# Three fixed tiles, used in turn, for the sums and tangents of an additive attention layer

## The chip, the cores and the metric

The kernel runs on one core of a Trainium2 chip. The core has five engines that run their own instruction streams[...]: TensorE (PE, with its weight loads as PEld), VectorE (DVE), ScalarE (ACT), GpSimd (POOL) and SyncE (SP, which here issues the DMAs). The metric is the device time of one execution in microseconds, the median of several runs.

## The reference

A four-layer network over `x` of shape (4, 56, 56, 128): neighbourhood attention, a selective-scan block, then layer 2 and layer 3, each an attention and a mixture of experts over the 3136 tokens of an image. The change lies in the attention of layer 2, which is additive: a score is a weighted sum of 16 tangents, not a dot product.

```python
def _L2_attn_ref(x, W1, b1, w2, b2):              # x: normalized tokens (4, 3136, 128)
    f = einsum('bih,ha->bia', x, W1[:h])          # queries, a = 16
    g = einsum('bjh,ha->bja', x, W1[h:])          # keys
    t = tanh(f[:, :, None, :] + g[:, None, :, :] + b1)
    scores = einsum('bija,a->bij', t, w2[:, 0]) + b2[0]
    e = exp(scores) * tril(ones, -1)              # key j strictly before query i
    w = e / (sum(e, axis=-1, keepdims=True) + 1e-10)
    return einsum('bij,bjh->bih', w, x)           # then t = t + this
```

So every pair of a query and an earlier key of the same image needs 16 sums, 16 tangents and a weighted sum of them.

## The kernel before, in words

All in float32. The four images stay in SBUF (`X0` to `X3`, 28 tiles of 112 tokens each). Layer 2's attention (`layer2_attention`, L1139) works on one image after the other, and in an image on four chunks of 7 query tiles (784 queries). For a chunk, all keys up to its own last tile are gone through, one key tile `J` of 112 keys at a time, and each key tile in two halves. A half of a key tile is a *piece*; there are 560.

A piece holds 56 keys as 7 groups of 8 keys. In SBUF the 128 partitions of the tile `th` are 8 keys times 16 values of `a`, and its 7 x 784 elements per partition are 7 *slots* (one per group of keys) of 784 queries. A piece goes through four steps:

- `adds` (L1290), DVE: 7 instructions, one per slot, each writes slot `s` as the queries `fT` plus one column of keys `g` (L1297). On pieces whose keys lie among the chunk's own queries (the diagonal) only the columns `lo:hi` of each slot that come after the keys are made, so the instructions become narrower from 784 to 56 columns.
- `tangents` (L1302), ACT: one instruction takes the tangent of all 7 slots in place (L1306).
- `scores` (L1308), PE: for each slot and each half of 392 queries one matmul with the small matrix `place` sums over `a` with the weights `w2` and adds the rows of these keys to the PSUM tile `s` (L1320). The order is: slots 0 to 3 on the first 392 queries, slots 0 to 3 on the second, slots 4 to 6 on the first, slots 4 to 6 on the second. Where only the second half of the queries is left, it is slots 0 to 3, then 4 to 6.
- once both halves of a key tile are there: `weights` (L1329), ACT, takes the exponential (L1334, on the diagonal L1337), on the diagonal POOL multiplies by the mask `later` (L1341), and `weighted` (L1343), PE, adds the keys' tokens to the output `o` (L1350).

The order is written out by hand: the pools are under a manual schedule for PE, ACT, DVE and POOL, so each engine runs in the order of the program, and only SP's order is the scheduler's. For piece `i` the loop (L1435) issues: `tangents(i)`; perhaps one or two steps of background work (`deal`: normalizing and projecting the next chunk, the previous image's experts); `add_ahead(i + 2)`, which is `adds` of the piece two ahead; before the first half of a key tile `gather`, which is `weighted` of the key tile two before; `scores(i)`; after the second half `weights` of the key tile before. So DVE works two pieces ahead of ACT, and PE follows ACT in the same piece.

The tile `th` is made anew for each piece from the pool `sm` with three buffers (L1294). A new tile takes the buffer of the tile three pieces before. It may be written when the earlier tile has had its last access, whichever slot that was: the first of the seven adds of piece `i` waits for the last of the fourteen matmuls of piece `i - 3`. Before the seventh add the program then has no other wait on PE.

Where the tiles lie also matters in two places. The pools of layer 2 are opened in the order `l2_w`, `l2_big`, `l2_sm` (L1146 to L1153) and take the room that layer 1 gave back; layer 3's pools (L1798 on) take the room of layer 2 in the same order, beginning with the router's and the experts' weights `rw`, `ew`, `ew_last`, `rw_last` and the matrix `back` (L1800 to L1820). A tile of a later layer waits until the tiles that lay in its place have had their last access. By the addresses in the program of before, `ew` lies over `wf`, `wg` and the first of `l2_big`'s tiles, `xa` and `xT`; the three buffers of `th` lie behind all of `l2_big`, after `fT`.

Of the kernel before, what the change touches and what calls it, by code (L numbers as in the profile page):

```python
# [20 lines left out]
P = 128  # L21
TP = 2 * HW
# [35 lines left out]
NG = TP // JG  # L58
QW = 32

WT = 7
# [77 lines left out]
class Hybrid:  # L139
# [999 lines left out]
    def layer2_attention(self):  # L1139
# [5 lines left out]
        with ExitStack() as ctx:  # L1145
# [6 lines left out]
            big = ctx.enter_context(tc.tile_pool(name="l2_big", bufs=1, reuse_waits="tile"))  # L1152
            sm = ctx.enter_context(tc.tile_pool(name="l2_sm", bufs=2, reuse_waits="tile"))  # L1153
# [9 lines left out]
            self.psum2 = m, hold  # L1163
            pools = self.f2_wide, self.f2_sm, lambda: self.psum2[0](), lambda: self.psum2[1]()
            root = lambda var: self.rstd(sm, var, [TP, NT], 1e-5, "ln", bufs=1)
            im, fT, po, ps, th, es = {}, {}, {}, {}, {}, {}
            g, xk = {}, {}
            bind = lambda f, *args: lambda: f(*args)
# [10 lines left out]
            def span(j, J, half=0):  # L1179

                t, n = chunks[order[j][1]]
                return max(J - t, 0) * TP + (half * TP // 2 if J >= t else 0), n * TP
# [100 lines left out]
            def rounds(half):  # L1283

                return [
                    [(blk, 2 * half + q) for blk in range(3)] + ([(3, half)] if q == 0 else [])
                    for q in range(2)
                ]

            def adds(i):  # L1290
                j, J, half = pieces[i]
                lo, hi = span(j, J, half)
                b = order[j][0]
                th[i] = self.t(sm, [P, NG // 2, WT * TP], "th", bufs=3)  # L1294
                for s, (blk, q) in enumerate(sum(rounds(half), [])):
                    at = NG * (J % WT) + NG // 2 * half + 2 * blk + (q % 2 if blk < 3 else 0)
                    nc.vector.tensor_scalar(  # L1297
                        th[i][:, s, lo:hi], fT[j][:, lo:hi], g[b, J // WT][:, at : at + 1],
                        None, op0=ALU.add,
                    )  # L1300
# [90 lines left out]
            def add_ahead(i):  # L1391
                if i < len(pieces):
                    j = pieces[i][0]
                    if i == first[j] and j:
                        while now or later_on:
                            assert not state.held
                            run((now or later_on).pop(0))
                    adds(i)
# [808 lines left out]
```

## Time and profile before

| what | value |
|---|---|
| time, median of 3 runs | 7028.35 us (7022.07 to 7032.54) |
| the profiled execution's own time | 7027.59 us |
| its span, first to last instruction | 7025.8 us |
| DVE, ACT, PE busy over the span | 5763.3, 4832.9, 6054.1 us |
| layer 2's pieces, first add to last score | 3002.8 to 5601 us of the span |
| tangents, L1306 | 560, 2184.2 us; a full one 4785 ns |
| sums, L1297 | 3920, 1868.9 us; a full one 623 ns, of which the next covers the end |
| scores' matmuls, L1320 | 14112 rows, 1391.6 us |

Every matmul of float32 shows as two rows, so a full piece of 14 matmuls has 28. In the timeline view rows of one kind that follow each other without a gap are merged: "x28" on DVE is 28 instructions in one unbroken row. In the brackets stands how long the engine was idle before the row and what ended that. The view of waits gives, for an engine and a line, what it waited for: us in total, times, the longest. An engine's idle time costs nothing unless the engine that sets the pace waits in its turn.

### The profile page before, as it was taken

How to read it: one execution, taken by the hardware profiler on the slowest of the kernel's cores; microseconds unless marked ns; L12 is line 12 of the kernel's file. 1: busy time of each engine (PE TensorE's matmuls, PEld its weight loads, DVE VectorE, ACT ScalarE, POOL GpSimd, SP SyncE). 2: the span in 40 equal slices, each digit the busy share in tenths (PEclk: the TensorE clock that was granted, in tenths of full speed). 3: DMA queues.
4: the chain of work that ended last, by engine and by line, in shares of the span. 5: the costliest groups of instructions: out<-in, count | busy, mean ns of one | idle time of the engine just before them, and what ended most of it. 6: DMA issues, size and time to landing. Idle time of an engine off the chain costs nothing.

```text
span 7025.8 us, 101491 instructions
## 1 busy us (share of the span) xinstructions
PE 6054.1 (86%) x37386; PEld 2622.7 (37%) x37386; DVE 5763.3 (82%) x10108; ACT 4832.9 (69%) x4828; POOL 2849.9 (41%) x1921
## 2 busy tenths in 40 slices
PE   8889999999999999877777777777788799999998
PEld 7633333333233233232233323332333355555554
DVE  6879999999999999977878888888887753566665
ACT  5567667776766777589989998999899833322231
POOL 2369989998999999811010001000101100000000
PEclk9989989999999899889999999999899999999999
DMA  3057767777776777600000000000003304243433
GB/s 53 5 139 187 187 165 186 184 178 175 188 185 171 176 189 187 153 8 3 1 6 3 8 2 6 4 6 3 6 20 116 89 18 149 72 109 92 118 85 94
DMA packets 363447, 654.19 MB, mean 93 GB/s; under 512 B 95413, under 2 KB 211909, under 8 KB 362438
## 3 DMA queue, kind: packets, MB, share of 16 engines
q1 hardware_dynamic: 362949, 647.71, 36.9%
q8 instruction: 295, 4.83, 0.3%
q14 instruction: 203, 1.66, 0.1%
HBM read 536.78 MB, written 104.37 MB: 91 GB/s over the span
## 4 chain that ended last, share of the span: by engine, by line
PE 23%; ACT 12%; DVE 11%; issue 8%; POOL 1%; SPq 0%; DMA 0%; DVEq 0%; ACTq 0%; POOLq 0%
ACT th L1306 10%; PE o L1944 6%; DVE th L1297 6%; PE q L1932 5%; PE s L1320 5%; DVE X L2144 2%; PE pe L2139 2%; ACT e L1334 1%; POOL e L1341 1%; PE o L1350 1%; PE m L1478 1%; PE m L1253 1%; DVE wide L1964 1%; DVE X L1486 0%; PE m L1761 0%
## 5 line engine op out<-in xcount | busy, mean ns | idle before, releaser
L1306 ACT ACTIVATE th<-th 128x5488 f32<-128x5488 f32 (+13 forms) x560 | 2184.2, 3943 | 175.4 <-DVE th L1297 151.4
L1297 DVE TENSOR_SCALAR th<-fT,g 128x784 f32<-128x784 f32 (+13 forms) x3920 | 1868.9, 549 | 307.2 <-PE s L1320 286.5
L1320 PE MATMUL s<-th,place 128*32 128x392 f32 (+5 forms) x14112 | 1391.6, 488 | 442.2 <-ACT th L1306 439.5
L860 DVE TENSOR_TENSOR_SCAN hs<-E,u 128x896 f32<-128x896 f32 x728 | 1449.7, 2007 | 3.6 <-ACT E L844 3.6
L844 ACT ACTIVATE E<-E,rate 128x448 f32<-128x448 f32 x1456 | 886.0, 661 | 121.9 <-DMA E<-delta_dram 118.4
L865 POOL TENSOR_TENSOR hs<-hs,room 128x896 f32<-128x896 f32 x448 | 924.8, 2083 | 82.9 <-DVE hs L860 82.5
L865 POOL TENSOR_TENSOR hs<-hs,bc 128x896 f32<-128x896 f32 x448 | 926.5, 2087 | 47.3 <-DVE hs L860 45.6
L1320 PEld LDWEIGHTS s<-th,place 128*32 128x32 f32 (+1 forms) x14112 | 455.1, 111 | 1311.1 <-ACT th L1306 666.3
L1937 ACT ACTIVATE e<-q,shift 128x448 f32<-128x448 f32 (+1 forms) x511 | 322.0, 633 | 673.7 <-PE q L1932 653.4
L1341 POOL TENSOR_TENSOR e<-e,later 112x112 f32<-112x112 f32 x112 | 155.0, 1384 | 1131.4 <-ACT e L1334 676.6
L2144 DVE SCALAR_TENSOR_TENSOR X<-pe,r_gate,X 112x128 f32<-112x128 f32 x896 | 311.9, 348 | 309.6 <-PE pe L2139 273.5
L871 PE MATMUL y<-hs,sum 128*32 128x448 f32 x3584 | 499.4, 631 | 4.0 <-POOL hs L865 4.0
L1932 PE MATMUL q<-xT 128*128 128x448 f32 (+1 forms) x1022 | 501.3, 573 | 0.9 <-ACT e L1937 0.9
L1944 PE MATMUL o<-e,xk 128*128 128x448 f32 (+1 forms) x1022 | 479.2, 552 | 16.1 <-ACT oT L1909 16.1
L806 PE MATMUL u<-room,pick 32*128 32x448 f32 x1456 | 413.4, 638 | 68.5 <-DVE hs L860 66.7
L1350 PE MATMUL o<-e,xk 112*128 112x392 f32 (+5 forms) x1024 | 389.3, 500 | 91.8 <-POOL e L1341 88.2
L806 PE MATMUL u<-du,pick 32*128 32x448 f32 x1456 | 402.8, 618 | 74.2 <-DVE hs L860 72.9
L1237 POOL MEMSET xa<- 112x4 f32 (+1 forms) x32 | 55.1, 1723 | 969.9 <-PE m L1230 969.8
L853 DVE TENSOR_TENSOR u<-u,bc 128x896 f32<-128x896 f32 x364 | 391.8, 1076 | 26.1 <-PE u L806 25.8
L853 DVE TENSOR_TENSOR u<-u,room 128x896 f32<-128x896 f32 x364 | 391.8, 1076 | 22.0 <-PE u L806 21.9
L2073 POOL MEMSET lc_xa<- 112x4 f32 x28 | 3.1, 109 | 945.7 <-DVE lc_xa L2067 696.4
L848 ACT ACTIVATE u<-u 128x896 f32<-128x896 f32 x168 | 151.9, 904 | 297.3 <-PE u L797 218.1
(310 smaller groups left out, 8767.5 us busy)
## 6 DMA issues: line engine op xcount, KB each, us to landing
E<-delta_dram SPq DMA_DIRECT2D x728, 448.0 KB
V<-du_dram SPq DMA_DIRECT2D x168, 448.0 KB
wide<-in_L_ffn_weight SPq DMA_DIRECT2D x64, 1024.0 KB
r<-M SPq DMA_DIRECT2D x189, 224.0 KB
M<-wide SPq DMA_DIRECT2D x72, 392.0 KB
du_dram<-room SPq DMA_DIRECT2D x112, 112.0 KB
delta_dram<-room SPq DMA_DIRECT2D x112, 112.0 KB
du_dram<-du SPq DMA_DIRECT2D x112, 112.0 KB
```

Source lines behind the costliest of these rows:

```text
L806: nc.tensor.matmul(halves(to)[:, k], w["pick"][own, q, :], pre[j]["du"][own, f], start=True, stop=True,)
L844: nc.scalar.activation(e, e, AF.Exp, scale=rate)
L853: eng.tensor_mul(v, v, pre[p // PAIRS]["bc"][:, 0:1].to_broadcast([P, 2, CH]))
L860: nc.vector.tensor_tensor_scan(flat, E.pop(p), V.pop(p), 0.0, op0=ALU.mult, op1=ALU.add)
L865: nc.gpsimd.tensor_mul(HS[p], HS[p], bc[:, 1:2].to_broadcast([P, 2, CH]))
L871: nc.tensor.matmul(py[j, f][r * HD : (r + 1) * HD, :], w["sum"][:, q, :], HS[p + r // 2][:, r % 2], start=False, stop=(q == QG - 1),)
L1297: nc.vector.tensor_scalar(th[i][:, s, lo:hi], fT[j][:, lo:hi], g[b, J // WT][:, at : at + 1], None, op0=ALU.add,)
L1306: nc.scalar.activation(own, own, AF.Tanh)
L1320: nc.tensor.matmul(ps[j, J][QW * blk : QW * blk + rows, h, lo:hi], place[:, off : off + rows], z[:, at + s, h * HALF + lo : h * HALF + hi] ...
L1350: nc.tensor.matmul(po[j][:, h, lo:hi], xk[b, J // WT][:, J % WT, :], e[:, h * HALF + lo : h * HALF + hi], start=(J == 0), stop=(J == t + ( ...
L1932: nc.tensor.matmul(ps[:n, :CH], of_tile(xT[b], t), xT[b][:, c * CH : (c + 1) * CH], start=True, stop=True,)
L1944: nc.tensor.matmul(po[b, c], xk[b][:n, t, :], e[:n], start=first, stop=last)
```

## The change

The ring of three tiles is made once, ahead of the loop, in the pool `big`, and piece `i` takes tile `i` modulo 3 in place of a new tile of the pool `sm`.

```diff
             root = lambda var: self.rstd(sm, var, [TP, NT], 1e-5, "ln", bufs=1)
+            ring = [self.t(big, [P, NG // 2, WT * TP], f"th{i}") for i in range(3)]
             im, fT, po, ps, th, es = {}, {}, {}, {}, {}, {}
...
                 b = order[j][0]
-                th[i] = self.t(sm, [P, NG // 2, WT * TP], "th", bufs=3)
+                th[i] = ring[i % len(ring)]
                 for s, (blk, q) in enumerate(sum(rounds(half), [])):
```

The number of buffers, their size, the instructions and their order on PE, ACT, DVE and POOL stay as they are. What differs is how a buffer comes free. A fixed tile is never handed on as a whole; each access waits for the earlier accesses that overlap it. The add into slot `s` of piece `i` then waits for the tangent of piece `i - 3` and for those matmuls of piece `i - 3` that read slot `s`, so each of the seven adds has a wait on PE of its own in place of one wait ahead of all seven. And the ring lies elsewhere: it is the first thing made in `big`, so it comes ahead of `xa` and the rest of that pool, in the place where layer 3 later puts its weights.

## The prediction

> **What bounds the kernel now.** The change touches only layer 2's pieces, so I read the busy time of that stretch first, then who waits for whom in it, then the timeline at places where ACT idles.
>
> ```profile
> 3002.00:5605.00 2603.00, 1988.25 (x17139) 802.11 (x17138) 2154.44 (x4982) 2413.03 (x985) 262.99 (x254) 0.94 0.07 19
> ```
>
> The columns are the stretch, then busy us of PE, PEld, DVE, ACT and POOL, the granted PE clock and the DMA share. ACT is busy for 2413 of 2603 us; it sets the pace, and the most that any change of waits can give in this stretch is its 190 us of idle time. The view of waits for the same stretch says what that idle time is:
>
> ```profile
> DVE th L1297 <- PE s L1320: 286.5, 218, 6.7
> ACT th L1306 <- DVE th L1297: 151.4, 73, 8.0
> ...
> PEld s L1320 <- DVE th L1297: 37.2, 169, 0.5
> ```
>
> DVE waits 286.5 us for matmuls before its first add: this is the wait that the change makes finer. But only 151.4 us of ACT's time go into waiting for adds. The question is how much of the 151.4 stands behind a part of the 286.5. Two places of the timeline answer it. The steady state, in the middle of a chunk:
>
> ```profile
> 3260.64 3.85 DVE L1297 TENSOR_SCALAR th<-fT,g 128x784 f32<-128x784 f32 x7 [0.71 <-PE s L1320]
> ...
> 3262.53 9.44 ACT L1306 ACTIVATE th<-th 128x5488 f32<-128x5488 f32 x2
> ...
> 3267.36 2.83 PE L1320 MATMUL s<-th,place 128*32 128x392 f32 x28 [1.13 <-ACT th L1306]
> ...
> 3270.33 3.85 DVE L1297 TENSOR_SCALAR th<-fT,g 128x784 f32<-128x784 f32 x7 [1.62 <-PE s L1320]
> 3271.86 0.91 ACT L1334 ACTIVATE e<-s,b 112x784 f32<-112x784 f32 x1
> ...
> 3272.66 9.45 ACT L1306 ACTIVATE th<-th 128x5488 f32<-128x5488 f32 x2
> ```
>
> Two tangents (9.45) and one exponential (0.9, its end under the next tangent) repeat every 10.13 us with no bracket on ACT: it never idles. DVE needs 2 x 3.85 of the 10.13 and waits out the rest. Here its wait for PE is worth nothing. The other place is the step from one chunk to the next:
>
> ```profile
> 3170.98 12.66 DVE L1297 TENSOR_SCALAR th<-fT,g 128x56 f32<-128x56 f32 x28 [0.64 <-ACT e L1337]
> ...
> 3173.41 10.52 POOL L1341 TENSOR_TENSOR e<-e,later 112x112 f32<-112x112 f32 x1 [1.90 <-ACT e L1337]
> 3176.21 9.45 ACT L1306 ACTIVATE th<-th 128x5488 f32<-128x5488 f32 x2 [2.87 <-DVE th L1297]
> ...
> 3183.98 1.11 PE L1350 MATMUL o<-e,xk 112*128 112x224 f32 x2 [10.53 <-POOL e L1341]
> ...
> 3185.03 7.02 PE L1320 MATMUL s<-th,place 128*32 128x392 f32 x56
> ...
> 3189.55 3.85 DVE L1297 TENSOR_SCALAR th<-fT,g 128x784 f32<-128x784 f32 x7 [5.91 <-PE s L1320]
> ...
> 3193.52 4.78 ACT L1306 ACTIVATE th<-th 128x5488 f32<-128x5488 f32 x1 [2.96 <-DVE th L1297]
> ```
>
> POOL's mask product cannot move while DVE runs 28 adds without a break (10.52 us, against 0.42 to 0.62 elsewhere). PE stands behind it, runs 56 rows of scores late, DVE waits 5.91 for the first 28 of them, and ACT idles 2.96. Here DVE's wait is on the path.
>
> **The change, part by part.** *The finer wait.* A full piece's 28 rows start in 8 groups, 0.33 us apart (the weight loads at 3267.36, .72, 3268.05 and on). Slots 0 to 3 are the first four groups and are free after 3 x 0.33 + 0.49 (one matmul) = 1.48 us; the last slot after 7 x 0.33 + 0.49 = 2.80. The first add can go 1.32 us earlier. Slot 4 is wanted 4 x 0.54 = 2.2 us after slot 0 and is free 1.32 after it, so no second wait follows. I go through ACT's idle times, follow DVE's unbroken run back to what it waited for, and credit a place only where that was a score, with the smallest of ACT's gap, DVE's wait and the time between the two slots' last matmuls there (from the ends of the single matmuls).
>
> - Chunk steps, the second or third full-width piece: eight places, ACT gaps 2.5 to 3.8, DVE waits 5.7 to 6.7. PE has been idle and its clock is lower (0.85 in that window), so the earlier release is worth more: 2.36, 1.58, 1.53, 2.17, 2.09 on full pieces, 1.33, 1.65, 1.62 on narrower ones. Sum 14.3.
> - Three places one piece before a gap of 0.6: 1.8.
> - The last 56-column piece before a step, whose shift passes on to the next gap of 2.87: 7 x 0.345 + 3 x 0.14 + 0.4 = 3.3.
> - Narrow pieces where an image starts (3 x (0.39 + 0.56 + 0.47) + 0.2), at the very start (1.6) and at the end of layer 2 (0.94 + 1.09 + 0.57 + 0.38): 9.0.
>
> Together 28.4 us. The rest of ACT's idle time (8.03 at each image's start, 5.7 and 3.4 at others) follows runs of DVE that waited for PE's `m` matmuls or for nothing: the change does not reach it. A shift at one place is kept at the next, because ACT, DVE and PE of what follows hang on each other; that is an assumption, and if a wait for a DMA or an `m` matmul takes half of it back, 14 is left.
>
> *A rule that would give more.* The Trainium skill, "Perfetto Trace Analysis", section Optimization Strategy, says that the same gap repeating on the engine that should be saturated can mean that buffers are short. DVE's 0.71 and 1.62 repeat like that; read so, up to 286.5 us. But the rows show ACT without a gap there, so I take the rows: 28.4.
>
> *Six more waits per piece.* 3360 adds get a wait that is mostly met. The row of 28 adds at 3170.98 crosses three piece boundaries whose waits were met, and it is one unbroken row: its 21 full adds take 11.36 us, 0.54 each, as within a piece ((3.85 - 0.62) / 6). So a met wait costs 0. From the other side: if each made an add start only when the one before has ended, it costs 0.62 - 0.54 = 0.085. I count 832 adds in the DVE runs that end at an ACT gap; 6/7 of them x 0.085 = 61 us. I take 0, the nearest row. PE has to signal the ends of 7 slots separately; in the single rows the narrow pieces, where many matmuls signal today, start as closely on each other as the others, 0. Below zero neither can go: no instruction is taken away.
>
> *A rule against the change.* The Trainium skill, "SBUF — State Buffer", section Who interferes with whom: a DVE instruction in a two-port mode and a GpSimd instruction shut each other out for the whole instruction. A DVE that waits less leaves POOL fewer openings. By the rule POOL waits for one add (0.54); by the row it waits for a whole run (10.52). But where ACT sets the pace DVE's idle time per piece is fixed by ACT, 2.4 us per two pieces, and only moves; at the chunk steps the run of 28 adds is there already and is followed by a wait of 4 us still. So 0. At worst a product comes later by one run of 3.85 us at the three widest key tiles of each of the 16 diagonals, which the two tangents of 4.8 that ACT still has ahead cover; were that cover gone, 48 x 3.85 = 185 us, of which nothing shows today.
>
> *The place of the ring.* Layer 3's weights now lie over the ring's first tile, so they wait for the last score that reads it (piece 558) instead of `xa`.
>
> ```profile
> 5580.36 0.43 SPq L164 DMA_DIRECT2D ew<-in_L_ffn_expert_w  x1
> ...
> 5600.14 0.78 PE L1320 MATMUL s<-th,place 128*32 128x112 f32 x28
> ...
> 5609.57 1.22 DVE L1809 TENSOR_TENSOR ew<-ew,ew_last 128x1024 f32<-128x1024 f32 x1
> ```
>
> The load goes from 5580.4 to about 5600.7; behind it on SP stand only `ew_last`, `rw_last` and `back`. The first use is DVE's subtraction at 5609.6, which layer 3's statistics follow. 1.05 MB at the 200 GB/s that the windows from 5580 to 5588 show is 5.3 us, with 1.5 for issue and start: landed at about 5608, hidden by 1 to 2 us of cover. With `rw_last`'s 4.4 us of issue, at worst 3 late. Below zero is excluded: the load is early today. I take +1. At the front, `xa` moves over layer 1's `hs` buffers; their last reader ends by 2979, `xa` is first written at 2984.9: 0.
>
> **Sum.** 7027.6 (the profiled execution) - 28.4 + 1 = 7000.2; it lies 0.8 under the median, so 7001.
>
> **Rivals.** (1) No effect, 7028: dependences might be kept per tile, not per slot. Against it: PE's 169 short waits for single adds (37.2 us, last line of the waits) can only be there if the parts of a tile are told apart. Also here: half of the gain given back, 7014. (2) Slower: met waits break the overlap of adds, 61 - 28 + 1, so 7062; it decides from 40 ns per wait on. The unbroken row of 28 speaks against it. (3) More: the waits break the run that shuts POOL out, and the rest of the gaps at the eight chunk steps goes too (24.8 - 14.3 = 10.5), 6990.
>
> **How the numbers follow.** A measurement of this kernel tells about 0.2% (14 us) from no change. Forecast, 6988 to 7014: 0.62; rival 3 and beyond: 0.06; rival 1 with the half: 0.21; rival 2 with POOL's delay and late weights: 0.11. Faster 0.68, same 0.21, slower 0.11. The range runs from 6985 (half as much again as the forecast gain) to 7035.
>
> **What would show it.** In the profile after: DVE's wait for scores well under 286.5, by some 0.8 to 1.3 at each first add; ACT's wait for adds near 125 in place of 151; the gap at the second chunk step about 1.4 in place of 2.96; no change in the 10.13 of the steady state; a full piece's adds still 3.85; `ew` issued near the last score. If ACT's wait is unchanged with DVE's wait shorter, the shift is not kept; if adds take over 4 us, rival 2 holds.

## The result and the profile after

The time fell from 7028.35 to 6980.64 us (median; 6973.61 to 6982.10), a ratio of 0.9934 with a 95% interval of 0.9924 to 0.9945: 47.7 us, where 27.4 were forecast. The profiled execution of after took 6973.61, its span is 6971.8; it is the quickest of its five, and 54.0 under the profiled one of before. Times here and below are medians; one execution of free_before (7190.74 us, at a granted clock of 0.845 where its others have 0.935 to 0.937) is left out of that kernel's figures.

First the stretch of layer 2's pieces of after, with the same columns as before (stretch, busy us of PE, PEld, DVE, ACT, POOL, clock, DMA share, GB/s), then its view of waits.

```profile
2993.00:5553.50 2560.50, 1990.54 (x17139) 804.21 (x17138) 2150.17 (x4980) 2411.12 (x985) 201.40 (x254) 0.94 0.06 19
```

```profile
DVE th L1298 <- PE s L1321: 228.5, 215, 4.3
ACT th L1307 <- DVE th L1298: 120.9, 65, 9.0
...
PEld s L1321 <- DVE th L1298: 33.8, 135, 0.5
PE o L1351 <- POOL e L1342: 31.5, 26, 10.5
```

The stretch is 42.5 us shorter. PE, DVE and ACT do the same work at the same clock. ACT's wait for adds fell from 151.4 to 120.9, about as forecast (125); by the pages its idle time ahead of tangents, whatever ended it, fell by more, from 175.4 to 134.9. DVE's wait for scores fell from 286.5 to 228.5, which is 0.27 for each of its 215 waits and not the 0.8 to 1.3 that the prediction gave as a sign. And POOL is busy for 201.4 us in place of 263.0, though its instructions are the same. The costliest groups of the two pages show the line that makes 51.4 of these 61.6, before and then after (the count, busy us and mean ns, then the idle time):

```profile
L1341 POOL TENSOR_TENSOR e<-e,later 112x112 f32<-112x112 f32 x112 | 155.0, 1384 | 1131.4 <-ACT e L1334 676.6
```

```profile
L1342 POOL TENSOR_TENSOR e<-e,later 112x112 f32<-112x112 f32 x112 | 103.6, 926 | 1176.0 <-ACT e L1335 666.0
```

The mask product is held up less. Before, eight of these products took 9.9 to 10.5 us, one at each of the eight chunk steps; after, only the first does. (The products away from these eight steps took 87 us in all in place of 73.) The timeline of after at the step shown in the prediction:

```profile
3156.30 12.86 DVE L1298 TENSOR_SCALAR th<-fT,g 128x56 f32<-128x56 f32 x28 [0.72 <-PE s L1321]
...
3158.74 0.86 POOL L1342 TENSOR_TENSOR e<-e,later 112x112 f32<-112x112 f32 x1 [1.41 <-ACT e L1338]
...
3161.72 9.45 ACT L1307 ACTIVATE th<-th 128x5488 f32<-128x5488 f32 x2 [3.07 <-DVE th L1298]
...
3166.56 8.39 PE L1321 MATMUL s<-th,place 128*32 128x392 f32 x56 [6.26 <-ACT th L1307]
...
3169.49 2.24 DVE L1298 TENSOR_SCALAR th<-fT,g 128x784 f32<-128x784 f32 x4 [0.33 <-PE s L1321]
...
3171.31 9.44 ACT L1307 ACTIVATE th<-th 128x5488 f32<-128x5488 f32 x2
```

The row of 28 adds is there as before (12.86 us, 0.20 longer). POOL's product comes 2.44 us into it, as before (2.43), but takes 0.86 in place of 10.52. So PE follows the first of the two tangents directly (3166.56, when it ends) and is no longer late; DVE waits 0.33 for its scores in place of 5.91; and ACT's gap of 2.96 has gone altogether, where the forecast left 1.4. In mid-chunk the pace did not change, as forecast: two rows of ACT in the same place follow each other at 3243.29 and 3253.42, 10.13 apart, and a full piece's adds still show 3.85.

```profile
3243.29 9.44 ACT L1307 ACTIVATE th<-th 128x5488 f32<-128x5488 f32 x2
...
3244.27 3.85 DVE L1298 TENSOR_SCALAR th<-fT,g 128x784 f32<-128x784 f32 x7 [0.82 <-PE s L1321]
...
3248.12 2.83 PE L1321 MATMUL s<-th,place 128*32 128x392 f32 x28 [1.11 <-ACT th L1307]
...
3249.73 3.85 DVE L1298 TENSOR_SCALAR th<-fT,g 128x784 f32<-128x784 f32 x7 [1.61 <-PE s L1321]
...
3252.62 0.91 ACT L1335 ACTIVATE e<-s,b 112x784 f32<-112x784 f32 x1
...
3253.42 9.44 ACT L1307 ACTIVATE th<-th 128x5488 f32<-128x5488 f32 x2
```

The finer wait itself can be read here. The first add that waits for a row of scores starts 1.61 us after that row begins (3249.73 and 3248.12); before, it was 2.97 (3270.33 and 3267.36 in the prediction's rows). That is 1.36 earlier, where 1.32 was worked out. DVE's idle time does not shrink by it: 0.82 and 1.61 are again the 2.43 that two pieces of 3.85 leave of ACT's 10.13. So the add is done earlier and waits longer for the next release, which is why DVE's wait in all fell so little.

### The profile page after: what moved, and what is told of

It reads as the page before. It is cut to its first block, busy times and chain, and to the rows that moved or that the text cites. A ratio compares the mean times of both kernels' runs of the same rounds, so it can differ in the third digit from the quotient of the medians.

```text
span 6971.8 us, 103016 instructions
## 1 busy us (share of the span) xinstructions
PE 6049.8 (87%) x37386; PEld 2622.0 (38%) x37386; DVE 5761.4 (83%) x10108; ACT 4832.3 (69%) x4828; POOL 2786.7 (40%) x1921
## 4 chain that ended last, share of the span: by engine, by line
PE 23%; DVE 12%; ACT 11%; issue 11%; POOL 1%; DMA 1%; SPq 0%; DVEq 0%; ACTq 0%; POOLq 0%
ACT th L1307 9%; PE o L1945 6%; DVE th L1298 6%; PE q L1933 5%; PE s L1321 5%; DVE X L2145 2%; PE pe L2140 2%; ACT e L1335 1%; PE o L1351 1%; PE m L1254 1%; DVE wide L1965 1%; PE m L1479 1%; PE m L1762 0%; DVE X L1487 0%; POOL e L1342 0%
## 5 line engine op out<-in xcount | busy, mean ns | idle before, releaser
L1307 ACT ACTIVATE th<-th 128x5488 f32<-128x5488 f32 (+13 forms) x560 | 2182.5, 3946 | 134.9 <-DVE th L1298 120.9
L1298 DVE TENSOR_SCALAR th<-fT,g 128x784 f32<-128x784 f32 (+13 forms) x3920 | 1864.9, 548 | 234.0 <-PE s L1321 228.5
L1342 POOL TENSOR_TENSOR e<-e,later 112x112 f32<-112x112 f32 x112 | 103.6, 926 | 1176.0 <-ACT e L1335 666.0
```

The costliest lines, as they stand in the source:

```text
L1298: nc.vector.tensor_scalar(th[i][:, s, lo:hi], fT[j][:, lo:hi], g[b, J // WT][:, at : at + 1], None, op0=ALU.add,)
L1307: nc.scalar.activation(own, own, AF.Tanh)
```

## The experiments

Theory 1: the waits per slot make the gain, and part of it comes through POOL's product, which gets in between the adds. Its rivals: waits on every add, even met ones, open the run for POOL (rival 3 of the prediction); or it is the ring's place in SBUF. "Held" is a mask product of over 9 us, anywhere in the layer; a product at a chunk step is named by the first piece of the new chunk (14, 42, 84 and so on). "Gap" is ACT's idle time ahead of one tangent at each of the eight chunk steps (pieces 17, 45, 87, 143, 227, 283, 367 and 423, counted from 0), from the profiles. Ratios are to the executions of before that were timed beside each kernel (7027.4 and 7028.3 us), not to the 7028.35 of the result:

| kernel | median us | gap at the eight steps | sum | held |
|---|---|---|---|---|
| before | 7028.4 | 3.76 2.96 2.92 2.48 3.58 2.81 3.49 2.77 | 24.8 | 8 |
| after | 6980.6 | 1.34 0 0 0 0 0 0 0 | 1.3 | 1 |
| ring_whole | 7029.8 | 3.77 2.97 2.93 2.49 2.69 2.47 2.62 2.46 | 22.4 | 11 |
| ring_old_place | 6980.6 | 1.33 0 0 0 0 0 0 0 | 1.3 | 1 |
| whole_at_56 | 6998.7 | 1.33 1.50 1.34 1.09 1.34 1.10 1.34 1.08 | 10.1 | 9 |
| whole_but_56 | 7019.1 | 3.89 3.34 3.34 2.94 3.83 3.19 3.83 0 | 24.4 | 7 |
| mask_pe_before | 7002.0 | 0 0 0 0.28 0.02 0.39 0 0 | 0.7 | none left |
| mask_pe_after | 6981.4 | 0 0 0 0 0 0 0 0 | 0 | none left |

**ring_whole: the ring without the finer wait.** The add into the slot that PE reads last goes first.

```diff
-                for s, (blk, q) in enumerate(sum(rounds(half), [])):
+                slots = list(enumerate(sum(rounds(half), [])))
+                for s, (blk, q) in slots[-1:] + slots[:-1]:
```

> The ring stays, but the first add of a piece writes the slot that is read last, so it waits for the whole tile; the other six adds keep a wait in the instruction that is always met. Theory 1, the finer wait makes the gain (and what follows from it): back to the time of before, 7028 within 5, POOL's mask product held for about 10 us at eight chunk steps again. Theory 2, a wait on every add, though met, opens the run of adds for POOL: the products take under 1 us and some 10 us of the 48 stay, 7018. Theory 3, it is the ring's place or the missing pool: no change from after, 6981.

7029.80 us, 1.0007 of before (0.9998 to 1.0015): all of the gain is gone. Its view of waits in layer 2:

```profile
DVE th L1299 <- PE s L1322: 294.4, 221, 6.7
ACT th L1308 <- DVE th L1299: 159.2, 82, 8.0
```

Both are back at, or a little over, the values of before (286.5 and 151.4). The other six adds have a wait in the instruction here too, at 357 of the 560 pieces by the trace (on DVE's own earlier adds, always met), and 11 products were held, eight at these steps and three at others. So neither the ring nor met waits on the adds bring anything; theory 2 falls.

**ring_old_place: the ring where the tangents lay before.**

```diff
-            ring = [self.t(big, [P, NG // 2, WT * TP], f"th{i}") for i in range(3)]
+            ring = [self.t(sm, [P, NG // 2, WT * TP], f"th{i}", bufs=1) for i in range(3)]
```

> The three fixed tiles are taken from the pool where the tangents lay before, so addresses are as before and the waits as after. Theories 1 and 2: 6981 within 5; layer 3's expert weights are loaded at their early time again, which moves the end by less than 2 (my estimate of that cost was 1). Theory 3, the place of the ring: back towards 7028.

6980.62 us (0.9931; 0.9919 to 0.9944), as after. The place has no effect that can be measured; theory 3 falls.

**whole_at_56 and whole_but_56: the finer wait at some pieces only.** In the first the pieces of 56 columns go back to the wait for the whole tile, in the second all the others do.

```diff
+                for s, (blk, q) in slots[-1:] + slots[:-1] if hi - lo == TP // 2 else slots:     # whole_at_56
+                for s, (blk, q) in slots[-1:] + slots[:-1] if hi - lo > TP // 2 else slots:      # whole_but_56
```

> As after, but the pieces of 56 columns wait for their whole tile. Theory 1 with the addition that whether POOL gets in is set by when the product arrives within the train of adds, which the 56-column piece starts: the product is held for about 10 us at seven chunk steps again although every full-width add still has its own wait; about 1.4 us of gap comes back at each, with 3.6 of the 56-column pieces themselves: 6981 + 9.8 + 3.6 = 6994. Theory 2, the waits on the adds open the run: products stay under 1 us, only the 3.6 comes back, 6985.

6998.67 us (0.9955; 0.9943 to 0.9968): 18.0 over after, where 13 were expected. Between the two profiles layer 2 is 13.6 longer, as expected; the other 4 are not explained. The same chunk step in its timeline:

```profile
3161.82 12.66 DVE L1299 TENSOR_SCALAR th<-fT,g 128x56 f32<-128x56 f32 x28 [1.26 <-ACT e L1339]
...
3164.26 10.50 POOL L1343 TENSOR_TENSOR e<-e,later 112x112 f32<-112x112 f32 x1 [1.90 <-ACT e L1339]
...
3178.79 4.02 DVE L1299 TENSOR_SCALAR th<-fT,g 128x784 f32<-128x784 f32 x7 [4.31 <-PE s L1322]
...
3182.91 4.78 ACT L1308 ACTIVATE th<-th 128x5488 f32<-128x5488 f32 x1 [1.50 <-DVE th L1299]
```

POOL is shut out again for 10.50 us although each of the 21 full-width adds has its own wait on PE: the waits do not open the run. And with POOL shut out, the finer wait does what the prediction worked out: DVE waits 4.31 in place of 5.91, ACT's gap is 1.50 in place of 2.96. Over the eight places ACT's tangents move up by 2.43, 1.46, 1.58, 1.39, 2.23, 1.71, 2.15 and 1.68 us: 14.6, where the prediction had 2.36, 1.58, 1.53, 1.33, 2.17, 1.65, 2.09 and 1.62: 14.3.

> As after, but every piece wider than 56 columns waits for its whole tile; only the 56-column pieces have the finer wait. Theory 1 with the arrival: the product gets in within 1 us at seven chunk steps as in after, PE is not late, and the gap at the chunk step goes even with the whole wait: 7028 - 3.6 - 7 x 2 to 3 us = about 7006 (7003 to 7012). Theory 2: like ring_whole, 7018 or, if whole waits hold POOL out, 7024.

7019.13 us (0.9988; 0.9981 to 0.9995): neither 7006 nor the 7024 of theory 2. Two chunk steps of the same execution, pieces 42 and 420:

```profile
3171.01 10.53 POOL L1343 TENSOR_TENSOR e<-e,later 112x112 f32<-112x112 f32 x1 [1.41 <-ACT e L1339]
...
3191.51 4.78 ACT L1308 ACTIVATE th<-th 128x5488 f32<-128x5488 f32 x1 [3.34 <-DVE th L1299]
...
4932.69 0.42 POOL L1343 TENSOR_TENSOR e<-e,later 112x112 f32<-112x112 f32 x1 [1.40 <-ACT e L1339]
...
4945.05 7.80 ACT L1308 ACTIVATE th<-th 128x4704 f32<-128x4704 f32 x2
```

Where the product is held, the gap is 3.34; where it gets in, two tangents follow each other without a gap, though the wait is for the whole tile. So what I expected of a product that gets in was right, but not that it would: six of the steps where after lets it in held it all the same, though the 56-column piece ahead has the finer wait. The two kernels together say that at these steps this wait is needed to let it in (whole_at_56 is without it) and is not enough (whole_but_56 has it).

**mask_pe: no product on POOL at all.** The mask's zeros become -30000 (`later` less 1, times 30000) and PE adds them to the scores ahead of the exponential.

```diff
+                for h, (lo, hi) in masked.items():          # the diagonal's columns, by halves
+                    nc.tensor.matmul(ps[j, J][:TP, h, lo:hi], self.ident[:TP, :TP],
+                                     later[:, lo + h * HALF - cut : hi + h * HALF - cut],
+                                     start=False, stop=True)
...
-                    nc.gpsimd.tensor_mul(e[:, lo : lo + TP], e[:, lo : lo + TP], later)
```

> The kernel before, with POOL's mask product replaced by matmuls that add -30000 to the masked scores. Theory 1 (the lock at the chunk step is one of two causes of the gap there, the whole-tile wait the other, and either one taken away leaves little): the gaps of 2.5 to 3.8 at the eight chunk steps go although the wait is for the whole tile; 24.8 us of gap, some of it needed for the mask matmuls: 7028 - 20 to 30, about 7003. Theory 2, the finer wait alone is worth 47.7 whatever POOL does: gaps stay at 1.3 or more, 7015 or later.

7001.98 us (0.9962; 0.9949 to 0.9974), 1 from the forecast. The chunk step:

```profile
3168.58 12.49 DVE L1297 TENSOR_SCALAR th<-fT,g 128x56 f32<-128x56 f32 x28 [0.76 <-PE s L1325]
...
3183.19 3.86 DVE L1297 TENSOR_SCALAR th<-fT,g 128x784 f32<-128x784 f32 x7 [2.11 <-ACT th L1306]
3183.22 9.44 ACT L1306 ACTIVATE th<-th 128x5488 f32<-128x5488 f32 x2
```

With the whole-tile wait of before, and no product, ACT has no gap: DVE's add waits for ACT, no longer for PE. So the whole-tile wait makes no gap here without a held product, and taking the product away is enough to remove the 24.8 us.

> The kernel after with the same mask matmuls. The only product of after that is still held over 9 us is the first one; its gap of 1.34 goes, and the products of 3.6 to 6.4 elsewhere cost little: 6981 - 2 to 6, about 6977. Then the finer wait without POOL's lock is worth 7003 - 6977 = 26, near the 28.4 of the sum. Theory 2: 47 between the two kernels.

6981.36 us (0.9931; 0.9917 to 0.9945), not under after and 4 over the forecast: the gap of 1.34 went, and no more was to be had. The finer wait without POOL's lock is worth 20.6 us by the medians and 25.6 by the two profiles (first to last tangent 2568.8 and 2543.2), against 26 expected.

**free: nothing on POOL beside the pieces.** The ones column of `xa` is set by DVE as well.

```diff
-                    nc.gpsimd.memset(r["xa"][:, :w, C - 1 : C], 1.0)
+                    nc.vector.memset(r["xa"][:, :w, C - 1 : C], 1.0)
```

> The kernel before with the mask matmuls, and with the ones column of xa set by DVE in place of POOL, so that POOL has nothing to do beside the pieces. POOL's memsets of 23 and 30 us there held back only the transfers of xk: 2 to 6 less than with the mask matmuls alone, about 6999.

> The kernel after with both. DVE's short waits for the transfer of xk (0.3 to 0.6 at four pieces) go, 32 memsets of 0.1 on DVE come: 2 to 6 less than with the mask matmuls alone, about 6973, and the quickest of all here. The finer wait's worth without POOL is then 26, as between the two kernels with the mask matmuls alone.

6995.6 us (0.9956; 0.9942 to 0.9969) and 6985.73 us (0.9941; 0.9929 to 0.9954): 6.4 under and 4.4 over the kernels with the mask matmuls alone, where 2 to 6 under was expected of both, and within the 8 to 14 us by which executions of one such kernel differ. The memsets' place is worth nothing that shows. By the profiles the finer wait is worth 24.6 here, by the medians 9.9; the two profiled executions are the slowest and the quickest of their kernels, so the larger figure is not the safer one. None of these kernels beats after by more than the noise.

**Three kernels once more, unchanged.**

> The kernel before, unchanged, for a second look at the products. If the program fixes who gets in, the eight products at the chunk steps are held about 10 us again and those of the pieces 182, 322, 462 and 504 get in within 1 us, 7028; if each execution draws anew, another set.

> The kernel after, unchanged, a second look. If the program fixes it: only the first chunk step's product (piece 14) is held 10 us, the other seven 0.86 each, 6981. If each execution draws anew: several of the seven held, 1.4 us of gap for each.

> The kernel whose times spread most (7006 to 7029), a second look. If the spread is POOL's draw: another set of steps with the product held than in its first profile (piece 420 alone got in there), and each that gets in takes about 2.9 us off; if the program fixes it, the same set and a time near 7019.

7031.81, 6974.55 and 7027.19 us. In each the products at the chunk steps came out as the first time: before held the same eight and let in those of pieces 182, 322, 462 and 504; after held that of piece 14 alone; whole_but_56 held the same seven and let in that of piece 420. So who gets in repeats, in the two profiled executions of each. The spread of whole_but_56's times (7006 to 7029) stays open: both of its profiled executions lie in the slower half (7022.17 and 7027.19), and whether more products get in when it is quick is not known.

## Why the prediction was right or wrong, point by point

The numbers are what the tangents move up between the profiled executions of before and after, in us, a gain being positive; in brackets those of the second pair of executions. The first two rows together are 24.1 (23.5). The 56-column pieces stand in the prediction as 3.3; its terms add up to 3.2.

| term | predicted | measured |
|---|---|---|
| chunk steps, finer wait alone (whole_at_56) | 14.3 | 14.6 |
| chunk steps, the product gets in | 0 | 9.5 |
| pieces 21, 49, 91, 231, 371 | 0 | 5.9 (5.9) |
| one piece before a gap of 0.6 | 1.8 | 1.9 (3.0) |
| 56-column pieces | 3.2 | 5.0 (5.0) |
| first pieces of the layer | 1.6 | 1.3 (1.3) |
| narrow pieces where an image starts | 4.5 | 5.2 (5.2) |
| end of the layer and all the rest | 3.0 | -1.3 (-2.2) |
| layer 2, first to last tangent | 28.4 | 42.1 (41.7) |

**The finer wait** was sized rightly: 14.6 against 14.3 at the chunk steps, each place within 0.12. ACT's wait, the 10.13 of the steady state and the 3.85 of a piece are as the prediction said. The sign on DVE's wait (0.8 to 1.3 less at each first add) was not: it contradicts the prediction's own "fixed by ACT, 2.4 us per two pieces", which held. A second wait within a piece, which the prediction excluded, came at eight pieces (2.5 us in all; the row of x4 in the result's first timeline is one).

The price of six more waits is nothing that shows, as predicted; by the instructions of after they are at 504 of the 560 pieces, 3024 adds in place of 3360, 2844 of them on PE. In the table, 2.7 of the 5.0 of the 56-column pieces came at three steps (182, 322, 462) where the next piece gives about as much back, in the last row. The rule on repeating gaps would have given up to 286.5; DVE's 0.7 to 1.6 in mid-chunk were worth nothing, as read.

**The step that failed is the one on POOL**: "at the chunk steps the run of 28 adds is there already and is followed by a wait of 4 us still. So 0." The run is there still, but at seven of the eight steps it no longer shuts the product out; PE is not late, and the rest of the gap goes. That is 9.5 us put at 0. Rival 3 named this place and about this size (10.5) at 0.06 and for a wrong reason: waits on the adds do not let POOL in (ring_whole, whole_at_56).

The reading under that 0, "POOL's mask product cannot move while DVE runs 28 adds without a break (10.52 us, against 0.42 to 0.62 elsewhere)", does not hold for before itself. Of its other 104 products 22 took 0.63 to 4.16. And at four more chunk steps (pieces 182, 322, 462 and 504) the product went through in 0.83 in the same kind of run, and ACT has no gap three pieces on, with the whole-tile wait. Before, at piece 182:

```profile
3813.22 12.84 DVE L1297 TENSOR_SCALAR th<-fT,g 128x56 f32<-128x56 f32 x28 [1.51 <-PE s L1320]
...
3815.67 0.83 POOL L1341 TENSOR_TENSOR e<-e,later 112x112 f32<-112x112 f32 x1 [1.27 <-PE s L1320]
...
3828.74 9.44 ACT L1306 ACTIVATE th<-th 128x5488 f32<-128x5488 f32 x2
```

So the profile of before has both outcomes, with a gap of 2.5 to 3.8 at the eight steps where the product is held and none at the four where it gets in; the prediction counted the eight and put a change of outcome at nothing. Between the Trainium skill's rule ("SBUF — State Buffer", Who interferes with whom: shut out for the other's instruction) and the row (10.52) I took the row for every place. The rows of after show both ends: 0.86 where POOL follows one add, as the rule has it, and 10.51 at piece 14, where it comes in the third of 21 full-width adds and is shut out through the 19 that are left, which overlap by 0.08 each. Taking only one end, with nothing kept for the other, is what made the range too short.

**A second, smaller term failed**: "credit a place only where that was a score". Four pieces after a chunk step ACT had a gap of 1.07, and the run of DVE behind it waited for PE's `m`, so I left it out. Before:

```profile
3210.10 0.16 DVE L1482 TENSOR_SCALAR den<-m 112x2 f32<-112x2 f32 x1 [0.88 <-PE m L1478]
...
3214.99 4.79 ACT L1306 ACTIVATE th<-th 128x5488 f32<-128x5488 f32 x1 [1.07 <-DVE den L1482]
```

But those matmuls stand on PE behind scores, which hang on the adds of the late pieces; the whole chain ran late against ACT. After, the same tangent is the second in one row (3191.58, 9.46 for two). In whole_at_56, with the product held, the five gaps are gone as well (5.9), so the finer wait alone closes them; in mask_pe_before, with the whole-tile wait, four of the five are gone too, so a chain that is not late closes them as well. A gap that hangs on a late chain is a second instalment of the first.

**"A shift at one place is kept at the next"** held in the sum. What I had for the layer's end (3.0) is not seen there: over the last seven pieces after lost 2.1 in the first pair of executions and gained 1.2 in the second. Such steps of 0.3 to 3.3 occur at some thirty pieces outside the other rows and largely cancel; two executions of after alone differ by 1.64 at pieces 27 and 55.

**The ring's place** was put at +1 and costs nothing that shows at the end. `ew` is loaded at the last score, as said, and its first use now waits 0.37 us for the loads behind it, where before it waited for none:

```profile
5550.02 0.37 SPq L164 DMA_DIRECT2D ew<-in_L_ffn_expert_w  x1
...
5558.72 1.23 DVE L1810 TENSOR_TENSOR ew<-ew,ew_last 128x1024 f32<-128x1024 f32 x1 [0.37 <-DMA ew_last<-in_L_ffn_expert_w]
```

From the last tangent to the end it is 1426.7 and 1423.8 us before, 1424.0 and 1423.9 after, and 1425.2 with the ring in its old place.

**Rival 1** falls, and its half is passed. **Rival 2** (overlap of adds lost) is not seen: the adds start 0.54 apart as before. The prediction's fear for POOL, fewer openings elsewhere, does show, as 87 us in place of 73, but it costs nothing that shows: mask_pe_after, without any product, is not faster than after.

**What stays open.** Of the 54.0 between the two profiled executions, layer 2 gives 42.1, what runs ahead of its first tangent 9.2 and what runs behind 2.7. Ahead of it nothing in the order of the instructions differs, and the first tangent fell between 2996.6 and 3012.3 in the thirteen profiles; I take the part of the 47.7 that is not layer 2's to be that spread, which no run shows. Open too is what decides whether POOL gets in. It is not the moment of arrival as the trace shows it: 0.04 to 0.05 us after an add's start it got in at seven places of after and was held at six of whole_but_56; at 0.06 to 0.07 it was held at seven places of before and got in at four. Nor is it the adds' waits: with them the product was held (whole_at_56), without them it got in (four steps of before). A delay put ahead of the product was not tried.

## What to carry to other kernels

Where one gap has two causes in a row (a product held up, then a wait for a whole tile), taking either away can close it, and the two gains do not add: here 24.8 us of gap fell to 0.7 without the product, to 10.1 with the finer wait alone, and to 1.3 with both eased. Size a finer wait by the time between the first and the last read of the buffer, and only where the engine that sets the pace idles; that was right to 0.3 us in 14.6. But any change to the timing of a long run on DVE can let a GpSimd instruction in, or shut it out, so keep both ends of that row in the range.

## What the runs showed of the hardware

A product of 0.42 us on GpSimd was held for 10.5 us, through 19 adds of 0.62 on VectorE that follow each other without a break, and got in after one add (0.83 to 0.86) in other runs of the same adds. Which of the two it is came out the same in both profiled executions of three programs; neither the moment of arrival within an add (0.04 to 0.07 us after its start in both cases) nor waits in the adds tell it beforehand. Six met semaphore waits per 3.85 us of adds cost nothing that shows.
